# Transforms of the 3x3 convolutions' input emitted at wider gaps in a two-layer attention and convolution kernel

## The chip, the cores and the metric

The kernel runs on one core of a Trainium2 chip. The time is device microseconds of one execution; three executions of the kernel before have a median of 3188.08 us, and lie between 3178.91 and 3189.95 us. The profiled execution is a run of its own. The engines are named as the profile names them: PE is TensorE (PEld its weight loads), DVE is VectorE, ACT is ScalarE, POOL is GpSimd, SP issues the DMAs.

## What is computed

Eight images of 512 channels by 32 x 32 pixels go through two layers, in float32. Layer 0, cut to what matters here:

```python
x = x + conv_ref(gn(x))                # layer 0; gn: GroupNorm, 32 groups
t  = silu(bn(conv1x1(gn_x, cv1)))      # 512 channels, two halves of 256
ys = [t[:, :256], t[:, 256:]]
for i in range(2):                     # two blocks
    yi = ys[-1]
    z  = silu(bn(conv3x3(yi, m_cv1[i])))
    q, k, v = conv1x1(z, qkv[i])       # 4 heads of 64
    a  = softmax(q.T @ (k + r) / 8)    # over 1024 pixels
    z  = silu(bn(conv1x1(v @ a.T, m_cv2[i])))
    ys.append(yi + z)
out = silu(bn(conv1x1(concat(ys), cv2)))
```

Layer 1 is a GroupNorm and a 1x1 convolution whose weights are scaled, masked and permuted by tables; its result is added to its input.

## The kernel before

**Slots.** The work on an image's block is called here by image and block: "2_1" is image 2, block 1. The attention of one block is a slot; the slots run in the order 0_0, 1_0, 0_1, 1_1, 2_0, 3_0, 2_1, 3_1, 4_0 and so on. A slot has four units (two head pairs by two halves of the queries). A unit goes through eight key tiles t, two to a softmax step: on VectorE `soften` (L545, adds the negated maximum), on ScalarE `exponent` (L549), on GpSimd the sums (L556), on TensorE `values` (L563) of the two tiles before and `logits` (L511) of the next unit. The next unit's logits are copied out of PSUM by ScalarE (L518) and their running maximum `mx` is taken by VectorE (L523). Between two units `top` transposes mx (L531) and reduces it to `nm` (L532), `spread` writes it out into `mb` (L540); `finish` and `divide` (L577 to L586) end the unit before. A softmax step takes about 9.2 us in the trace.

**What fills TensorE between.** `slot_filler` builds a list of other work for each slot: the 3x3 convolution (`conv3`) and the projections (`project`) of the next slot, the 1x1 convolution after the attention (`conv_m2`), and a background queue (`bg`) of cv1, cv2 and layer 1 (L175, with the results cv2s and xr at L130 and L457 and x2r at L487). After each softmax step the filler runs until its share of the slot is done. A `Clock` adds up estimated costs as this work is emitted; a call placed with `clock.at(delay, f)` is emitted when the clock has passed that time. So all delays and gaps in this text are estimated us of TensorE's work, and decide only where in the program an instruction stands.

**The transform.** A 3x3 convolution is done as six products over transformed planes of four rows (`conv3`, L297 on). `transform` makes the planes from `ybuf`, the padded input, with eight VectorE instructions in this order: a (L280), b (L281), plane 1 (L282), plane 2 (L283), a2 (L285), b2 (L286), plane 3 (L287), plane 4 (L288). Planes 0 and 5 are begun on GpSimd (L343, L344) and ended on VectorE (L345, L346). The eight are handed to a `Spread`: number n is due at delay + gap x n. `conv3` forces three of them out before its first product (`upto(3)`), the fourth before the second (`upto(4)`), all before it goes on from the second product (`upto(8)`). Two calls of `transform` stand in `slot_filler`: for block 1 of the next slot (L924), and for block 0 of the slot after the next (L939). Two more, for block 0 of images 0 and 1, stand ahead of the slots, outside it.

**Orders that are kept.** `in_turn` chains the mx, the softens and the transforms on VectorE in the order in which they are emitted; `act_turn` and `pe_turn` do the same for copies and exponentials on ScalarE and for the attention's matmuls on TensorE. All other instructions are placed by the framework's own scheduling, with the same in-order queues. All matmuls of the filler and the logits share one pool of five PSUM banks (`bank`): a matmul that starts a bank waits until the one who read its contents before is done.

Of the kernel before, what the change touches and what calls it, by code (L numbers as in the profile page):

```python
# [39 lines left out]
def conv_preact_kernel(ctx: ExitStack, tc: tile.TileContext, x, cv1, cv2, mcv1, qkv, mcv2, bn, rw, rh, conv, s_in, t_in, out):  # L40
# [698 lines left out]
    slots = []  # L739
# [157 lines left out]
    def call(f, *a):  # L897
        f(*a)
        return
        yield  # L900

    def finishing(im):


        bg.add(Second(im, 0), Second(im, 1), held.pop(), Last(im, 0))
        held.append(Last(im, 1))
        bg.prepare()

    def slot_filler(s):

        prev = slots[s - 1] if s else (None, 0)
        nxt = slots[s + 1] if s + 1 < len(slots) else (None, 0)
        todo, needed = [], 0.0

        def add(us, g):
            nonlocal needed
            todo.append((us, g))
            needed += us

        im, i = nxt  # L920
        add(8.0, bg.take(8.0))
        if im and i == 1:
            add(7.0, im.conv_m2(0))
            add(0.0, call(im.transform, 1, 3.0, 1.0))  # L924
            add(9.0, bg.take(9.0))
        products = im.conv3(i) if im else iter(())
        if prev[1] == 1:
            if im:
                add(21.3, (us for _, us in zip(range(16), products)))
            add(7.0, prev[0].conv_m2(1))  # L930
            add(0.0, call(lambda: finishing(prev[0])))
        if im:
            add(10.7 if prev[1] == 1 else 32.0, products)
            add(7.0, bg.take(7.0))
        if im:
            add(21.0, im.project(i))
        if s + 2 < len(slots) and slots[s + 2][1] == 0:
            add(0.0, call(slots[s + 2][0].load_y))
            add(0.0, call(slots[s + 2][0].transform, 0, 8.0, 1.3))  # L939
        rest = SHARE - needed if im else 70.0  # L940
        if rest > 0:
            todo.append((rest, bg.take(rest, wait=True)))
        total = sum(c for c, _ in todo)
        return needed, total, todo
# [76 lines left out]
    before = None  # L1021
    for s in range(len(slots)):
        needed, total, todo = slot_filler(s)
        state = {"done": 0.0}

# [66 lines left out]
    im = images[NB - 1]  # L1092
# [55 lines left out]
```

## Time and profile before

| | us |
|---|---|
| median of three executions | 3188.08 |
| the profiled execution's own time | 3188.51 |
| its span, first to last instruction | 3186.8 |
| TensorE busy in the span | 3085.9 |
| VectorE busy | 2050.6 |
| ScalarE busy | 1717.3 |
| GpSimd busy | 1395.3 |

The mean granted TensorE clock is 0.993. The group rows that this text speaks of, from the page (busy us, mean ns of one, idle of the engine just before and who ended most of it):

```profile
L556 POOL TENSOR_TENSOR sum<-sum,st 128x256 f32<-128x256 f32 x1536 | 1126.1, 767 | 570.1 <-ACT st L549 565.0
L523 DVE TENSOR_TENSOR mx<-mx,lg 128x512 f32<-128x512 f32 x768 | 477.8, 681 | 412.2 <-ACT st L518 412.2
...
L545 DVE TENSOR_TENSOR st<-st,mb 128x1024 f32<-128x1024 f32 x512 | 603.7, 1213 | 63.6 <-PE mb L540 63.6
L313 PE MATMUL m<-plane,w_m 128*128 128x256 f32 x2304 | 537.4, 388 | 21.8 <-DVE x2r L487 9.0
```

Sixteen transforms run, of eight instructions each. Matmuls overlap in the records, so a busy TensorE isn't TensorE at its peak, and a wait counts for the time only where TensorE itself stands.

### The profile page before, as it was taken

The page shows a single profiled execution, that of the slowest core. Times are in us where ns is not written, and L with a number is a line of the kernel's source. Part 1 is how long each engine was busy: PE and PEld are TensorE (multiplying, and loading weights), DVE is VectorE, ACT ScalarE, POOL GpSimd, SP SyncE. Part 2 cuts the span into 40 slices and gives each one's busy share as a digit, 9 for nine tenths or more (in the row PEclk, how much of TensorE's full clock was granted, in tenths as well). Part 3 has the DMA queues.
Part 4 walks back from the last instruction along what each step waited for, and adds up shares of the span by engine and source line. Part 5 has one row for each costly group of instructions (what it writes and reads, how often), then busy time and mean ns, then how long its engine had stood idle before and what let it go on. Part 6 is the DMA issues. An engine that isn't in the chain of part 4 may idle for free.

```text
span 3186.8 us, 34171 instructions
## 1 busy us (share of the span) xinstructions
PE 3085.9 (97%) x11668; PEld 1522.9 (48%) x11668; DVE 2050.6 (64%) x2718; ACT 1717.3 (54%) x2347; POOL 1395.3 (44%) x1867
## 2 busy tenths in 40 slices
PE   7999999999999999999999999999999999999999
PEld 3645444454445454454445454454445454453333
DVE  5446576667666676667666676667766676666742
ACT  3255765854655555544656455554656455555631
POOL 2114444446444454445444454355434454455420
PEclk9999999999999999999999999999999999999999
DMA  8851442421233232424233332424233332413366
GB/s 294 287 187 63 154 161 83 149 79 65 88 109 129 93 119 70 148 86 137 89 109 129 119 114 75 139 83 142 90 113 132 110 122 71 145 63 129 110 212 216
DMA packets 142014, 399.35 MB, mean 125 GB/s; under 512 B 13072, under 2 KB 14352, under 8 KB 141840
## 3 DMA queue, kind: packets, MB, share of 16 engines
q1 hardware_dynamic: 141120, 396.94, 36.4%
q8 instruction: 92, 1.51, 0.2%
q14 instruction: 82, 0.67, 0.1%
q10 hardware_dynamic: 720, 0.23, 0.0%
HBM read 317.42 MB, written 79.69 MB: 125 GB/s over the span
## 4 chain that ended last, share of the span: by engine, by line
PE 70%; DVE 7%; ACT 5%; issue 3%; DMA 2%; POOL 1%; ACTq 0%; DVEq 0%; SPq 0%; POOLq 0%
PE m L313 14%; PE cv L175 12%; PE lg L511 11%; PE po L563 11%; PE qk L175 6%; PE l L175 6%; PE v L405 3%; PE m L175 2%; DVE st L545 2%; PE mb L540 2%; ACT st L518 2%; PE mt L531 2%; PE den L577 2%; DVE mx L523 1%; ACT st L549 1%
## 5 line engine op out<-in xcount | busy, mean ns | idle before, releaser
L556 POOL TENSOR_TENSOR sum<-sum,st 128x256 f32<-128x256 f32 x1536 | 1126.1, 767 | 570.1 <-ACT st L549 565.0
L523 DVE TENSOR_TENSOR mx<-mx,lg 128x512 f32<-128x512 f32 x768 | 477.8, 681 | 412.2 <-ACT st L518 412.2
L549 ACT ACTIVATE st<-st 128x1024 f32<-128x1024 f32 x512 | 539.1, 1068 | 340.2 <-DVE st L545 338.8
L518 ACT COPY st<-lg 128x512 f32<-128x512 f32 x1024 | 524.4, 596 | 351.7 <-PE lg L511 306.6
L545 DVE TENSOR_TENSOR st<-st,mb 128x1024 f32<-128x1024 f32 x512 | 603.7, 1213 | 63.6 <-PE mb L540 63.6
L313 PE MATMUL m<-plane,w_m 128*128 128x256 f32 x2304 | 537.4, 388 | 21.8 <-DVE x2r L487 9.0
L556 POOL TENSOR_TENSOR sum<-st,st 128x256 f32<-128x256 f32 x256 | 188.0, 766 | 789.4 <-ACT st L549 789.3
L563 PE MATMUL po<-st,v 128*64 128x512 f32 x2048 | 500.3, 608 | 21.7 <-ACT st L549 14.7
L511 PE MATMUL lg<-q,k 64*128 64x512 f32 x2048 | 513.7, 619 | 1.6 <-ACT y L130 1.5
L313 PEld LDWEIGHTS m<-plane,w_m 128*128 128x128 f32 x2304 | 433.0, 192 | 149.0 <-issue 44.1
L175 PE MATMUL cv<-y,w_cv 128*128 128x512 f32 x1024 | 465.4, 599 | 10.8 <-DVE mx L523 6.2
L511 PEld LDWEIGHTS lg<-q,k 64*128 64x128 f32 x2048 | 178.6, 187 | 330.1 <-issue 266.4
L175 PEld LDWEIGHTS cv<-y,w_cv 128*128 128x128 f32 x1024 | 185.7, 190 | 251.7 <-issue 227.8
L563 PEld LDWEIGHTS po<-st,v 128*64 128x64 f32 x2048 | 128.9, 137 | 327.5 <-issue 228.9
L175 PE MATMUL l<-x,w_l 128*128 128x512 f32 x512 | 235.8, 603 | 10.3 <-DVE mx L523 10.0
L175 PE MATMUL cv<-x,w_cv 128*128 128x512 f32 x512 | 233.4, 603 | 8.5 <-ACT x L165 2.4
L175 PE MATMUL qk<-z,w_qkv 128*128 128x512 f32 x512 | 234.0, 600 | 1.7 <-DVE mx L523 1.7
L584 DVE RECIPROCAL rb<-rb 128x256 f32<-128x256 f32 x128 | 215.4, 1723 | 30.6 <-ACT rb L580 30.5
L532 DVE TENSOR_REDUCE nm<-mt 128x4 f32<-128x512 f32 x128 | 82.4, 685 | 158.6 <-PE mt L531 158.5
L580 ACT COPY rb<-den 128x512 f32<-128x512 f32 x64 | 37.3, 583 | 226.9 <-PE den L577 226.9
L175 PEld LDWEIGHTS l<-x,w_l 128*128 128x128 f32 x512 | 92.7, 190 | 132.3 <-issue 107.2
L175 PEld LDWEIGHTS cv<-x,w_cv 128*128 128x128 f32 x512 | 94.3, 192 | 126.4 <-issue 107.3
(145 smaller groups left out, 2404.3 us busy)
## 6 DMA issues: line engine op xcount, KB each, us to landing
w_m<-w_m SPq DMA_DIRECT2D x96, 768.0 KB, 4.8
w_cv<-in_cv SPq DMA_DIRECT2D x90, 512.0 KB, 3.5
y<-y SPq DMA_DIRECT2D x64, 512.0 KB, 4.4
x<-in_x SPq DMA_DIRECT2D x56, 512.0 KB, 5.4
y<-y SPq DMA_DIRECT2D x64, 256.0 KB, 3.5
k<-r SPq DMA_DIRECT2D x32, 512.0 KB, 3.6
res<-y SPq DMA_DIRECT2D x32, 512.0 KB, 4.0
xr<-in_x SPq DMA_DIRECT2D x32, 512.0 KB, 4.0
```

What stands on the lines that cost most here:

```text
L175: nc.tensor.matmul(ps, w, moving, start=(n == 0), stop=(n == len(terms) - 1))
L313: nc.tensor.matmul(ps[:, ts(co, 256)].rearrange("p (t x) -> p t x", x=F), w[:, co, c, dx], u[:, 9 * c : 9 * c + 8, dx : dx + F], start=(j ...
L405: nc.tensor.matmul(ps[:, ts(j, P)], z[:, c, ts(4 * j4 + j, P)], w[:, c, 512 + P * hp : 512 + P * hp + P], start=(c == 0), stop=(c == IT - 1),)
L511: nc.tensor.matmul(lg[h], self.k[r, ts(t, P)], self.q[r, self.hp, ts(self.half, HALF)], start=True, stop=True)
L518: act_turn(nc.scalar.copy(st[:, h], lg[h]))
L523: in_turn(nc.vector.tensor_tensor(self.mx[:, h], so_far[:, h], lg[h], ALU.max))
L532: nc.vector.tensor_reduce(self.nm[:, h], mt, AX.X, ALU.max, negate=True)
L545: in_turn(nc.vector.tensor_tensor(st, st, flat(self.mb), ALU.add))
L549: act_turn(nc.scalar.activation(st, st, AF.Exp))
L556: nc.gpsimd.tensor_tensor(flat(self.acc)[:, part], flat(so_far)[:, part], st[:, part], ALU.add)
L563: nc.tensor.matmul(self.po[HD * h : HD * h + HD], self.v[:, t, ts(h, HD)], self.st[t][:, h], start=(t == 0), stop=(t == KT - 1),)
L584: nc.vector.reciprocal(self.rb[:, r], self.rb[:, r])
```

## The change

Two calls in `slot_filler` get another delay and gap. The transform of block 1 becomes due from 2.0 on at every 3.3 instead of from 3.0 on at every 1.0; that of block 0 from 8.0 on at every 3.3 instead of every 1.3. The eight instructions, what they compute and who reads them stay the same. All eight transforms of block 1 and six of block 0 (images 2 to 7) go through these calls; the two ahead of the slots are left as they were.

```diff
@@ -921,7 +921,7 @@
         add(8.0, bg.take(8.0))
         if im and i == 1:
             add(7.0, im.conv_m2(0))
-            add(0.0, call(im.transform, 1, 3.0, 1.0))
+            add(0.0, call(im.transform, 1, 2.0, 3.3))
             add(9.0, bg.take(9.0))
         products = im.conv3(i) if im else iter(())
         if prev[1] == 1:
@@ -936,7 +936,7 @@
             add(21.0, im.project(i))
         if s + 2 < len(slots) and slots[s + 2][1] == 0:
             add(0.0, call(slots[s + 2][0].load_y))
-            add(0.0, call(slots[s + 2][0].transform, 0, 8.0, 1.3))
+            add(0.0, call(slots[s + 2][0].transform, 0, 8.0, 3.3))
         rest = SHARE - needed if im else 70.0
         if rest > 0:
             todo.append((rest, bg.take(rest, wait=True)))
```

## The prediction

> **What bounds the kernel now.** I read the page's engine table first, then TensorE's list of waits, then the timeline and the table by stretch at each place where a moved transform runs.
>
> ```profile
> span 3186.8 us, 34171 instructions
> PE 3085.9 (97%) x11668; PEld 1522.9 (48%) x11668; DVE 2050.6 (64%) x2718; ACT 1717.3 (54%) x2347; POOL 1395.3 (44%) x1867
> ```
>
> TensorE is busy for 3085.9 of 3186.8 us. No matmul is added or removed, so what the change can win is part of the 100.9 us in which TensorE stands, plus matmuls that run at a lower clock. Who ends those waits:
>
> ```profile
> PE po L563 <- ACT st L549: 14.7, 12, 3.7
> ...
> PE l L175 <- DVE mx L523: 10.0, 5, 2.6
> PE m L313 <- DVE x2r L487: 9.0, 3, 3.5
> PE cv L175 <- DVE mx L523: 8.2, 7, 2.0
> PE m L313 <- ACT cv2s L130: 8.2, 3, 2.8
> ```
>
> (us in total, times, longest.) None of these is a wait for a transform's own plane. They are waits for PSUM banks that ScalarE or VectorE has not read out yet. The timeline around image 2, block 1 shows why (start, duration):
>
> ```profile
> 1136.49 1.14 DVE L280 SCALAR_TENSOR_TENSOR a<-ybuf 128x544 f32<-128x544 f32 x1
> ...
> 1137.55 1.25 DVE L281 SCALAR_TENSOR_TENSOR b<-ybuf 128x544 f32<-128x544 f32 x1
> ...
> 1138.83 1.14 DVE L282 TENSOR_TENSOR plane<-a,b 128x544 f32<-128x544 f32 x1
> ...
> 1139.88 0.71 DVE L283 TENSOR_TENSOR plane<-a,b 128x544 f32<-128x544 f32 x1
> ...
> 1140.52 2.34 DVE L545 TENSOR_TENSOR st<-st,mb 128x1024 f32<-128x1024 f32 x2
> ...
> 1141.76 1.06 ACT L549 ACTIVATE st<-st 128x1024 f32<-128x1024 f32 x1 [7.13 <-DVE st L545]
> ...
> 1142.84 1.28 ACT L130 ACT_TABLE_LOAD   x1
> ...
> 1144.13 0.78 ACT L130 ACTIVATE cv2s<-cv,bn_b,bn_s 128x512 f32<-128x512 f32 x1
> ...
> 1144.96 1.43 PE L313 MATMUL m<-plane,w_m 128*128 128x256 f32 x3 [2.71 <-ACT cv2s L130]
> ```
>
> Four transform instructions stand ahead of soften (L545). ScalarE has idled 7.13 us for it, then does the exponential, a table load and the activation that frees the bank; TensorE waits 2.71 us. The same pattern with other last steps stands at image 3, block 1, and image 4, block 0:
>
> ```profile
> 1333.24 3.07 PE L313 MATMUL m<-plane,w_m 128*128 128x256 f32 x13 [1.90 <-DVE x2r L487]
> ...
> 1457.88 2.41 PE L175 MATMUL l<-x,w_l 128*128 128x512 f32 x5 [1.83 <-DVE mx L523]
> ```
>
> And at image 3, block 0, where L287 and L288 stand ahead of the soften:
>
> ```profile
> 908.24 3.27 PE L175 MATMUL cv<-y,w_cv 128*128 128x512 f32 x7 [1.46 <-DVE mx L523]
> ```
>
> A long stall can cost twice. Three stretches from the table by stretch (us, busy times, then PEclk, the granted clock):
>
> ```profile
> 1862.00:1869.00 7.00, 6.22 (x15) 5.00 (x16) 5.58 (x9) 5.00 (x7) 4.71 (x5) 0.51 0.52 162
> 2053.00:2056.40 3.40, 3.40 (x10) 2.67 (x9) 2.03 (x4) 1.82 (x3) 3.30 (x6) 0.52 0.05 20
> ...
> 2583.00:2590.00 7.00, 6.14 (x32) 5.45 (x33) 5.88 (x10) 5.65 (x9) 4.71 (x5) 1.00 0.52 170
> ```
>
> The first and the last are the same stage for images 4 and 6, with nearly the same stall (2.87 and 2.78 us); after one the clock is half for about 6.8 us, after the other it is full. A half-clock stretch of 3.4 us loses about 1.7 us.
>
> **What the Trainium skill says.** "TensorE: Matmul & The Clock Gate", Part 1, "What's actually happening": the array falls to half clock after an idle window of about 3.4 us and rises after a busy one, and the window runs freely. The trace agrees with stretches of 3.4 and 6.8 us, and with images 4 and 6 differing; but here single stalls of 2.4 to 3.7 us already do it, sometimes, and among the moved places no single one of 2.1 us or less did (image 2's cluster below did). "PSUM — Partial Sum Buffer", "Engine vs sequencer instructions": the queues of ScalarE and VectorE are strictly first in, first out. The chain above is that. "SBUF — State Buffer", "Who interferes with whom": VectorE and GpSimd share one port pair as an exclusive lock. In the trace L286 takes 712 ns at the least and 1248 ns at the most, and the slow ones lie beside GpSimd's sums. "ScalarE: Activation LUTs", "What ACT_TABLE_LOAD costs": about 1283 ns and a drain; the trace has 1.28 us.
>
> **The change part by part.** Nothing is added or removed on any engine; SP's order is the same, so no DMA moves in its queue. GpSimd's list changes at one L343, at image 2. Of 16 transforms, 14 move: all eight of block 1, and block 0 of images 2 to 7. VectorE's order by program, image 2 block 1: before, L280 L281 L282 L283, soften 6, 7, L285 L286; after, L280 L281, soften 6, 7, L282, xr, then the four mx, L283 L285 L286 and the two nm. So each transform instruction that leaves the front of a soften brings it 0.71 (alone) to 1.25 us (beside sums) forward. A "stall" below is TensorE's lost time against its pitch, which is up to 0.2 us more than the idle in brackets.
>
> - *Images 2, 4, 6, block 1.* Stalls 2.78, 2.87, 2.78. L282 and L283 (1.14 + 0.71, less overlap) leave the chain: cv2s ends about 1.7 us earlier, 1.1 us of stall stays. 3 x 1.7 = 5.0. A stall of 1.1 should no longer drop the clock: 1.7 (image 2) and 3.4 (image 4), of which I take 3.4, as the window runs freely. Together 8.4.
> - *Images 3, 5, 7, block 1.* A first stall (2.40, 2.76, 1.71), ended by the mx behind ScalarE's norms, stays. The second (2.06, 3.71, 3.71) waits for x2r behind L285 to L288 and soften. After, L285 to L288 follow the four mx, and the program has this matmul wait for mx of step 6 instead, which should end about 1330.0 to 1330.7 against 1331.2 wanted at image 3, and up to 0.8 late at images 5 and 7. 2.06 + 2.9 + 2.9 = 7.9, with two half-clock stretches (2 x 1.65 = 3.3): 11.2. x2r is then needed one product later, 24 matmul records or 5.4 us, about 2.6 us after it is there.
> - *Images 4, 6, block 0.* 1.99 and 2.00: soften 4 (now at 1454.33 behind L285, L286, x2r, L287, L288) comes by 1450.9; mx then ends at 1455.6 at the latest against 1455.9 wanted. 4.0.
> - *Images 3, 5, 7, block 0.* 1.62, 1.63, 1.64 go for the same reason. But ScalarE's order turns there: the exponential of step 2 now precedes the table load and cv2s, which ends about 896.65 (before 892.76), while TensorE wants that bank at 895.66: a new stall of 1.0. Bounds -1 and +1.6 each; I take +0.6, so 1.9 in all.
> - *Image 0, block 1.* 1.65: mx should end at 439.3 against 439.05: 1.3. *Image 1, block 1.* 1.41, held by ScalarE's last activation, where one norm moves behind it: 0.4 (0 to 0.7).
> - *Image 2, block 0* (728 to 750). TensorE has too little work here: stalls of 1.36, 1.19 and 1.87 and half clock from 742.4 to 749.2. Soften 4 comes about 1.75 us earlier, soften 6 about 3 us. Bounds 1 and 6.5 (1.19 + 1.87 + 3.4); I take 4.0.
>
> Sum 8.4 + 11.2 + 4.0 + 1.9 + 1.3 + 0.4 + 4.0 = 31.2 us. What the moved instructions newly stand ahead of: in block 1 three or four of L283 to L288 now stand between the last mx and nm (L532). At image 3 VectorE's mx ends at 1335.57 and nm starts at 1339.38, and mb (L540), which needs nm, at 1342.35. Four at 1.25, x2r 0.63 and the small group-norm steps (about 1.1) fill 6.7 us, from an mx that ends near 1332.2: nm is done at 1340.2, and mb, 2.06 earlier than before, is wanted at 1340.3. The cover just suffices at the slow pace; at the quick pace 2 us are over. I cost it at nothing. The planes themselves have 3 us or more.
>
> The profiled execution took 3188.51 us for its span of 3186.8, and stands 0.43 over the median of 3188.08. 3188.5 - 31.2 = 3157.3; against the median 3157.
>
> **The rivals.** *The stalls move rather than go.* ScalarE's table loads and copies become last: each soften comes early, and its bank is still late, as at images 3, 5, 7, block 0. For it: the first stalls of images 3, 5, 7, block 1 already end so. Against: ScalarE idled 7.13 us before the exponential above. Only a third of the sum stays, about 10: 3178.
>
> *All go, with the lower clock.* The stalls listed are 8.4 + 9.5 + 4.0 + 4.9 + 1.65 + 1.41 + 4.4 = 34.3, half clock 5.1 + 3.3 + 3.4 = 11.8: 46 us, 3142. Against it: the table load stays in the chain.
>
> *Slower: a late nm.* In the eight block-1 windows L283 to L288 delay nm, so mb, and with it the whole next soften chain; the cover computed above was 0.1 us at the slow pace. If mx itself ends 2.5 us later than I think, each window loses 2.5 us, and with 6.8 us at half clock (3.4) 5.9: 8 x 5.9 = 47 against the 31 won, so +16: 3204. It decides from where nm ends more than 2 us later against mb than worked out. Against: before, VectorE idled 158.5 us over 128 nm.
>
> *The change doesn't do what it says.* conv3 forces three, then four, then all of the transform's instructions out (upto), which could undo the spacing. By the program's order it does not: no burst of more than three is left directly ahead of a soften. No change, 3188.
>
> **How the numbers follow.** Forecast (22 to 40 us won) 0.56; stalls move 0.24, of which a third still passes the bound; all go 0.12; slower 0.06; no effect 0.02. About 0.5% (16 us) is what a measurement of this kernel can tell from none: the three runs spread over 11 us. Faster 0.56 + 0.12 + 0.08 = 0.76, within 0.18, slower 0.06. The range 3138 to 3181 takes in the forecast, the larger gain and most of the moved stalls.
>
> **What would show it.** Right: soften 6 some 1.7 us earlier at image 2, block 1, with TensorE's wait near 1.1; "m L313 <- DVE x2r L487" gone from the waits; the waits of l and cv for mx down by 4 and 5; no half clock after 1862, 2053 and 2770; TensorE's idle near 78 us. Wrong: new waits of cv for cv2s over 1 us at images 3, 5, 7; waits of mb for nm; half clock at new places.

## The result, and the profile after

| | before | changed |
|---|---|---|
| median of six executions, us | 3188.59 | 3160.7 |
| lowest and highest | 3178.91, 3189.95 | 3156.5, 3164.71 |
| span of the profiled execution | 3186.8 | 3160.4 |
| TensorE busy | 3085.9 | 3078.6 |

The changed kernel takes 0.9918 of the time (95% interval 0.9907 to 0.993), 27.9 us less. Of the span's 26.4 us, 7.3 are TensorE's busy time (above all matmuls that no longer run at half clock) and 19.1 its idle time. TensorE's waits in the changed kernel (us in total, times, longest):

```profile
PE po L563 <- ACT st L549: 19.9, 17, 3.7
...
PE l L175 <- DVE mx L523: 6.0, 3, 2.3
PE cv L175 <- ACT cv2s L130: 4.6, 6, 0.8
PE cv L175 <- DVE mx L523: 4.5, 4, 2.7
...
PE m L313 <- ACT cv2s L130: 2.7, 3, 0.9
...
PE po L563 <- DVE mx L523: 0.8, 2, 0.4
```

The wait of m for x2r, 9.0 before, is gone; l and cv for mx fell from 10.0 to 6.0 and from 8.2 to 4.5; m for cv2s from 8.2 to 2.7. Two rows grew by more than 2 us: cv for cv2s, from 2.3 to 4.6, and po for the exponential, from 14.7 to 19.9. The second is mostly a change of name: po for mx fell from 6.9 to 0.8, and the two together from 21.6 to 20.7. Two rows of before that the comparison needs:

```profile
PE po L563 <- DVE mx L523: 6.9, 8, 2.3
...
PE cv L175 <- ACT cv2s L130: 2.3, 3, 0.8
```

The timeline at image 2, block 1, in the changed kernel:

```profile
1137.65 1.24 DVE L281 SCALAR_TENSOR_TENSOR b<-ybuf 128x544 f32<-128x544 f32 x1
...
1138.82 2.34 DVE L545 TENSOR_TENSOR st<-st,mb 128x1024 f32<-128x1024 f32 x2
1140.06 1.06 ACT L549 ACTIVATE st<-st 128x1024 f32<-128x1024 f32 x1 [5.33 <-DVE st L545]
...
1142.43 0.78 ACT L130 ACTIVATE cv2s<-cv,bn_b,bn_s 128x512 f32<-128x512 f32 x1
...
1143.26 3.08 PE L313 MATMUL m<-plane,w_m 128*128 128x256 f32 x13 [0.91 <-ACT cv2s L130]
```

Soften begins at 1138.82 instead of 1140.52, cv2s at 1142.43 instead of 1144.13: 1.70 us earlier each, and TensorE waits 0.91 us where it waited 2.71. The table by stretch at the two places of before that were shown at half clock (us, busy times of the five engines, then the granted clock, DMA share and GB/s):

```profile
1851.00:1858.00 7.00, 6.93 (x36) 6.15 (x37) 6.92 (x9) 4.88 (x8) 4.21 (x5) 1.00 0.73 227
2036.00:2039.40 3.40, 3.40 (x17) 2.86 (x16) 3.37 (x6) 0.63 (x1) 2.63 (x3) 1.00 0.90 275
```

Both have the full clock, and do 36 and 17 matmul records where half clock did 15 and 10. The next table is made from the start of the same matmul in both traces (TensorE runs the same matmuls, in the same order but for a few at image 2, block 0): how much a stretch of slots got shorter (-) or longer (+). The last column is a second profiled execution of the changed kernel (the ninth run below).

| stretch | forecast | first profile | second |
|---|---|---|---|
| images 2, 4, 6, block 1 | -8.4 | -8.6 | -7.7 |
| images 3, 5, 7, block 1 | -11.2 | -11.4 | -13.3 |
| images 4, 6, block 0 | -4.0 | -4.2 | -4.2 |
| images 3, 5, 7, block 0 | -1.9 | -2.7 | -1.3 |
| image 0, block 1 | -1.3 | -1.6 | -1.3 |
| image 1, block 1 | -0.4 | +0.3 | -0.7 |
| image 2, block 0 | -4.0 | -2.0 | -1.5 |
| all 14 places | -31.2 | -30.2 | -30.0 |
| ahead of the first moved transform | 0 | +4.2 | +3.5 |
| after the last | 0 | -0.6 | +5.4 |

Ahead of the first moved transform the two programs are the same, so the 4.2 us there are the spread between executions (the other profiles below stand between -0.6 and +8.7 there, against the same profile of before, and all eleven at +3.2 on the mean). Where the 5.4 of the last line come from is told at the end.

### The profile page after: what moved, and what is told of

Its sections match the earlier page's. It is cut to its first block, busy times and chain, and to the rows that moved or that the text cites. A ratio compares the mean times of both kernels' runs of the same rounds, so it can differ in the third digit from the quotient of the medians.

```text
span 3160.4 us, 34182 instructions
## 1 busy us (share of the span) xinstructions
PE 3078.6 (97%) x11668; PEld 1515.6 (48%) x11668; DVE 2041.5 (65%) x2718; ACT 1718.7 (54%) x2347; POOL 1398.7 (44%) x1867
## 4 chain that ended last, share of the span: by engine, by line
PE 75%; ACT 4%; DVE 3%; issue 2%; DMA 2%; POOL 1%; ACTq 0%; DVEq 0%; SPq 0%; POOLq 0%
PE cv L175 14%; PE m L313 13%; PE lg L511 12%; PE po L563 12%; PE l L175 7%; PE qk L175 6%; PE v L405 3%; PE m L175 3%; PE den L577 2%; PE mb L540 2%; PE mt L531 1%; ACT st L518 1%; POOL sum L556 1%; ACT st L549 1%; DVE st L545 1%
## 5 line engine op out<-in xcount | busy, mean ns | idle before, releaser
L313 PE MATMUL m<-plane,w_m 128*128 128x256 f32 x2304 | 528.7, 383 | 4.7 <-ACT cv2s L130 2.7
L563 PE MATMUL po<-st,v 128*64 128x512 f32 x2048 | 498.9, 605 | 20.7 <-ACT st L549 19.9
L313 PEld LDWEIGHTS m<-plane,w_m 128*128 128x128 f32 x2304 | 426.5, 189 | 129.0 <-issue 45.4
L175 PE MATMUL cv<-y,w_cv 128*128 128x512 f32 x1024 | 464.5, 599 | 8.6 <-ACT cv2s L130 4.6
L175 PEld LDWEIGHTS cv<-y,w_cv 128*128 128x128 f32 x1024 | 185.8, 190 | 248.9 <-issue 226.7
L175 PE MATMUL cv<-x,w_cv 128*128 128x512 f32 x512 | 235.6, 607 | 9.2 <-DVE mx L523 2.7
L175 PE MATMUL l<-x,w_l 128*128 128x512 f32 x512 | 236.5, 606 | 6.2 <-DVE mx L523 6.0
L175 PE MATMUL qk<-z,w_qkv 128*128 128x512 f32 x512 | 234.0, 600 | 1.3 <-DVE mx L523 1.3
L175 PEld LDWEIGHTS cv<-x,w_cv 128*128 128x128 f32 x512 | 95.0, 193 | 128.8 <-issue 107.6
L175 PEld LDWEIGHTS l<-x,w_l 128*128 128x128 f32 x512 | 93.1, 191 | 127.9 <-issue 110.3
```

The source lines that it names most:

```text
L175: nc.tensor.matmul(ps, w, moving, start=(n == 0), stop=(n == len(terms) - 1))
L313: nc.tensor.matmul(ps[:, ts(co, 256)].rearrange("p (t x) -> p t x", x=F), w[:, co, c, dx], u[:, 9 * c : 9 * c + 8, dx : dx + F], start=(j ...
L563: nc.tensor.matmul(self.po[HD * h : HD * h + HD], self.v[:, t, ts(h, HD)], self.st[t][:, h], start=(t == 0), stop=(t == KT - 1),)
```

## The experiments

Two theories went in. S: a transform instruction ahead of a soften delays by its length the exponential, the PSUM bank and the matmul behind it, and each place stands alone. Against it M (the stalls only move from engine to engine), D (the burst itself costs, wherever it stands), and, after the first four runs, A (ScalarE's order of cv2s and the exponential decides). "Soften 6" is the soften of key tile 6. Ratios are against the kernel before on the same chip. Stalls are counted as in the prediction, against TensorE's pitch (the usual time from one matmul's start to the next): 0.98 us is the stall where a bracket shows 0.91 of idle.

**One call at a time.** Each kernel is the kernel before with one of the two edits:

```diff
-            add(0.0, call(im.transform, 1, 3.0, 1.0))
+            add(0.0, call(im.transform, 1, 2.0, 3.3))
```

> Only the block-1 call has the new delay and gap (2.0, 3.3). Theory S (a transform instruction ahead of a soften delays the exponential, the bank and the matmul behind it, and each place stands alone): the block-1 places alone, about 21 us won against before (ratio 0.9934); stalls of images 2, 4, 6 near 1.0 instead of 2.8, the x2r waits of images 3, 5, 7 gone, and unchanged: 1.99 and 2.00 at images 4 and 6, block 0, and three of 1.6 at images 3, 5, 7, block 0. Rival M (the stalls move, and only the two edits together pay, since a later slot catches up): under 12 us won.

```diff
-            add(0.0, call(slots[s + 2][0].transform, 0, 8.0, 1.3))
+            add(0.0, call(slots[s + 2][0].transform, 0, 8.0, 3.3))
```

> Only the block-0 call has the new gap (8.0, 3.3). Theory S: about 9 us won (ratio 0.9972): the two stalls of 2.0 gone, the three of 1.6 gone against three new ones of 0.85 where cv2s comes late, 2 us at image 2; the block-1 stalls of 2.8 and 2.1 to 3.7 as before. Rival M: none or a loss, since the late cv2s at images 3, 5, 7 takes back what is won.

Block 1 alone: 3168.0 us against 3190.64, ratio 0.9931 (0.9911 to 0.995), 22.6 us won where S expected 21. Block 0 alone: 3182.21, ratio 0.9978 (0.9969 to 0.9986), 8.4 us won where it expected 9. The two ratios multiply to 0.9909, beside 0.9918 for both together: the parts add up, and M falls. With block 1 alone the x2r waits are gone and the stalls of 1.99 at images 4 and 6, block 0, stay; with block 0 alone the reverse. One detail missed: with block 1 alone the cv2s stalls of images 4 and 6 are 1.70, not 1.0. That does not belong to this edit: the changed kernel has the same 1.70 at image 6 in its second profile. There the additions that fill `ybuf` (L430) end 0.7 us later than in the first, counted from the mx before them, and with them a, b and soften.

**The burst, later.** The gaps of before, both bursts five later:

```diff
-            add(0.0, call(im.transform, 1, 3.0, 1.0))
+            add(0.0, call(im.transform, 1, 8.0, 1.0))
-            add(0.0, call(slots[s + 2][0].transform, 0, 8.0, 1.3))
+            add(0.0, call(slots[s + 2][0].transform, 0, 13.0, 1.3))
```

> The gaps of before (1.0 and 1.3), but both bursts begin five later (8.0 and 13.0), so that the burst stands behind soften 6, 7 at images 2, 4, 6 of block 1, and still five instructions ahead of soften 6 at images 3, 5, 7 and of soften 4 at images 4, 6 of block 0. Theory S (place against the soften counts, not the density): the cv2s stall of images 2, 4, 6 gone, but plane 1 is then late behind the four mx, so a wait of m for L282 of 3 us or more in its place; images 3, 5, 7 of block 1 and images 4, 6 of block 0 keep stalls of 2 us or more. Time within 15 us of before. Rival D (the density itself costs: a burst runs at the slow pace beside GpSimd's sums, wherever it stands): the stalls of images 2, 4, 6 stay with the same releaser, cv2s.

3210.2 us, ratio 1.0059 (1.0042 to 1.0075): 19.6 us slower, more than the 15 allowed. The timeline of this kernel, at image 2, block 1:

```profile
1155.21 0.73 DVE L282 TENSOR_TENSOR plane<-a,b 128x544 f32<-128x544 f32 x1
...
1156.04 6.24 PE L313 MATMUL m<-plane,w_m 128*128 128x256 f32 x20 [4.21 <-ACT st L549]
```

The bracket names ScalarE, but the matmul starts at 1156.04, 0.10 us after plane 1 (L282) ends at 1155.94: the first product needs plane 1, which now stands behind the four mx. The wait for cv2s has gone as S has it, and one for the plane has come. Images 3, 5, 7 have five transform instructions ahead of soften 6 and stalls of 5.9 to 6.4 us. D expected the wait for cv2s to stay; it didn't.

**All eight at once.**

```diff
-            add(0.0, call(im.transform, 1, 3.0, 1.0))
+            add(0.0, call(im.transform, 1, 3.0, 0.0))
-            add(0.0, call(slots[s + 2][0].transform, 0, 8.0, 1.3))
+            add(0.0, call(slots[s + 2][0].transform, 0, 8.0, 0.0))
```

> Gap 0 in both calls: all eight instructions at one place, begun where the kernel before begins them. Theory S: four more instructions, 2.9 to 5.0 us, ahead of soften 6 at images 2, 4, 6 of block 1: stalls of 5.7 to 7.8 us there; at images 4, 6 of block 0 soften 4 is free, so the 2.0 goes, but soften 2 is 4 to 7 us later and a wait appears one step earlier; the same at images 3, 5, 7 of block 1, where the x2r wait goes and the wait of l for mx grows. Sum 15 to 45 us slower than before. Rival M (TensorE waits for the end of each transform, however it is placed): the same time as before within 8 us.

3190.36 us, ratio 0.9999 (0.9988 to 1.001). S is wrong here: no stall of 5.7 to 7.8 us, and the waits of m for cv2s and for x2r are gone. ScalarE's and TensorE's timelines of this kernel, image 2, block 1, show why:

```profile
1155.92 0.78 ACT L130 ACTIVATE cv2s<-cv,bn_b,bn_s 128x512 f32<-128x512 f32 x1 [2.58 <-PE cv L175]
...
1161.85 1.06 ACT L549 ACTIVATE st<-st 128x1024 f32<-128x1024 f32 x1 [3.85 <-DVE st L545]
```

```profile
1159.60 5.45 PE L313 MATMUL m<-plane,w_m 128*128 128x256 f32 x24
1166.11 1.26 PE L531 MATMUL mt<-ident,mx 128*128 128x128 f32 x8 [1.06 <-DVE mx L523]
```

With soften so late, the program has cv2s ahead of the exponential on ScalarE. cv2s follows the matmuls that fill its bank directly, the product starts without a wait, and only the transposes of mx wait, 1.06 us. This suggests that what stands ahead of soften costs TensorE through ScalarE's order, and that this order is a second lever; the next runs test it. The cost moved: po waits for exponentials, 14.7 us before, for 32.9 here. The time is the one that rival M named, but not for the reason it gave: no product waits for a plane in this profile.

**ScalarE's order alone.** cv2s is not in the chain that `act_turn` writes out. One edit puts it there, where it is emitted, ahead of the exponential of the same step:

```diff
-                    bn_silu(t, ps, BN_CV2 + co)
+                    act_turn(nc.scalar.activation(t, ps, AF.Silu, bias=bn_b[:, BN_CV2 + co : BN_CV2 + co + 1], scale=bn_s[:, BN_CV2 + co : BN_CV2 + co + 1]))
```

First on the kernel before, no transform moved:

> The transforms stand where the kernel before has them; alone the activation cv2s (L456) is put into ScalarE's written order, so that it stands ahead of the exponential of the same step. Theory A (the stalls of images 2, 4, 6, block 1, come from the order on ScalarE: the exponential, which waits for soften, stands ahead of the table load and cv2s): the three cv2s stalls of 2.8 us gone or under 1 without any transform moved, 8 to 13 us won there with the half clock, less up to 4 us for six more table loads; the x2r waits of images 3, 5, 7 (2.1 to 3.7), the 2.0s of images 4, 6 and the 1.6s of images 3, 5, 7, block 0, stay. Ratio 0.997 to 0.999. Theory S (the transform ahead of the soften is the cause whatever ScalarE's order): stalls of 2 us or more stay there, ratio 1.000 or more.

3181.02 us against 3187.37, ratio 0.9977 (0.9969 to 0.9985). Image 2, block 1, in this kernel (ScalarE, then TensorE):

```profile
1139.78 0.78 ACT L456 ACTIVATE cv2s<-cv,bn_b,bn_s 128x512 f32<-128x512 f32 x1 [1.62 <-PE cv L175]
...
1142.98 1.06 ACT L549 ACTIVATE st<-st 128x1024 f32<-128x1024 f32 x1 [1.12 <-DVE st L545]
```

```profile
1143.46 4.80 PE L313 MATMUL m<-plane,w_m 128*128 128x256 f32 x21
```

The exponential still waits for soften, which still stands behind four transform instructions, but cv2s is done 2.4 us before it, and the product starts without a wait. So it is at images 4 and 6: all three cv2s stalls are gone. Instead the transposes of mx stall there by 0.8 to 1.3 us and mb by 0.8, and the x2r stalls of 3.7 us stay. Theory A holds for these places, and S only as long as ScalarE has the exponential ahead of cv2s. Then on the changed kernel:

> The changed kernel with the same edit. Theory A: the remaining 0.98s of images 2, 4, 6 and the new 0.85s of images 3, 5, 7, block 0, go, 5.5 us won against the changed kernel (about 3155), less what six more table loads of 1.28 us cost if they come onto the path (up to 7.7). Theory S: the 0.98s and 0.85s stay, no gain.

3150.52 us, ratio 0.9885 (0.9868 to 0.9902). ScalarE and TensorE at image 2, block 1, in this kernel:

```profile
1139.05 0.78 ACT L456 ACTIVATE cv2s<-cv,bn_b,bn_s 128x512 f32<-128x512 f32 x1 [1.62 <-PE cv L175]
...
1141.14 1.06 ACT L549 ACTIVATE st<-st 128x1024 f32<-128x1024 f32 x1
```

```profile
1142.72 5.45 PE L313 MATMUL m<-plane,w_m 128*128 128x256 f32 x24
```

ScalarE loads the table for cv2s at 1136.14, while it would wait for the convolution anyway; the exponential comes some 0.6 us later than in the changed kernel (0.33 us after the logits' start at 1140.81; there 0.31 ahead of 1140.37); and the product starts without a wait. The stalls of 0.85 at images 3, 5, 7, block 0, are gone too, and of the six added table loads TensorE sees little: its wait of cv for m2s is 3.4 us in four places instead of 2.1 in one.

**Other gaps.** 5.0, then 2.0, in both calls, with the changed kernel's delays:

```diff
-            add(0.0, call(im.transform, 1, 2.0, 3.3))
+            add(0.0, call(im.transform, 1, 2.0, 5.0))
-            add(0.0, call(slots[s + 2][0].transform, 0, 8.0, 3.3))
+            add(0.0, call(slots[s + 2][0].transform, 0, 8.0, 5.0))
```

> Gap 5.0 in both calls, else as the changed kernel; ScalarE's order is that of the changed kernel. Theory S with late planes: one instruction fewer ahead of soften 6 at images 2, 4, 6, but plane 1 (L282) stands behind the four mx and is 4 to 5 us late for the first product: waits of m for L282 of 3 to 5 us at images 2, 4, 6 of block 1, and planes 3 and 4 behind soften 0, 1 and the divides are late by 1 to 3 us at images 3, 5, 7. 15 to 30 us slower than the changed kernel, about the time of before. Rival (the further apart the better): as fast as the changed kernel or faster.

> Gap 2.0 in both calls, with the changed kernel's delays. Theory S: three instructions ahead of soften 6 at images 2, 4, 6 (two in the changed kernel, four before): stalls of 1.7 to 2.1; at images 4, 6 of block 0 three and x2r stand ahead of soften 4: about 1.5; x2r waits of 1 to 2.5 at images 3, 5, 7. 8 to 18 us won against before (0.9944 to 0.9975). Rival (only the step from four to two counts): the time of before within 5 us.

Gap 5.0: 3187.75 us, ratio 1.0 (0.9988 to 1.0011): the whole gain is given back. Its timeline at image 2, block 1:

```profile
1153.59 0.72 DVE L282 TENSOR_TENSOR plane<-a,b 128x544 f32<-128x544 f32 x1
...
1154.41 5.93 PE L313 MATMUL m<-plane,w_m 128*128 128x256 f32 x19 [4.61 <-ACT st L549]
```

Again the product starts 0.10 us after plane 1 ends. Stalls of 4.0 to 5.4 us stand at all five such places, images 1, 2, 4, 6 of block 1 and image 2 of block 0; those for planes 3 and 4 at images 3, 5, 7 did not come.

Gap 2.0: 3179.57 us, ratio 0.9976 (0.9968 to 0.9985), 7.8 us won (4.8 to 10.2 by the interval) where S expected 8 to 18 and its rival less than 5, so the time alone does not decide between them. Two rows of its waits:

```profile
PE m L313 <- ACT cv2s L130: 6.2, 3, 2.1
...
PE mb L540 <- DVE nm L532: 4.9, 5, 1.6
```

The stalls do decide. At images 2, 4, 6, with three instructions ahead of soften 6, the stall is 2.15; with two (the changed kernel) 0.98, with four (before) 2.78: each one counts. At images 3, 5, 7 x2r still stands behind soften and TensorE idles 3.5 us for it, more than the 1 to 2.5 expected: there it is not the number that counts, but whether the program lets the first product wait for mx and only the second for x2r. The stalls of about 1.5 expected at images 4 and 6, block 0, did not come. And a wait came that nobody expected here: at images 2 and 6 of block 1 mb idles 1.31 us for nm, behind L285 to L288.

In block 1 the change moves the delay too, from 3.0 to 2.0. With the delay of 2.0 the gaps 2.0, 3.3 and 5.0 win 7.8, 27.9 and nothing, so the delay alone does not make the gain; 3.0 with gap 3.3 was not run.

**Both kernels again, side by side on one chip.**

> The changed kernel again, beside the next run on the same chip: ratio to before 0.9907 to 0.993 as measured; cv2s stalls of 0.98 at images 2, 4, 6 and of 0.85 at images 3, 5, 7, block 0.

> The changed kernel with cv2s ahead of the exponential, again, on the same chip as the run above. Theory A: 0.15 to 0.35% faster than the changed kernel beside it (ratio to before 0.987 to 0.990), and the 6.3 us wait of gv_b at 3023 us was chance (GpSimd's sums in the way of one small VectorE instruction): absent here, with a profiled time near 3150. Rival: the wait belongs to the order, comes again, and the gain over the changed kernel is within the spread.

The changed kernel 3160.56 us (0.9915, 0.9901 to 0.9929); with cv2s first 3152.51 (0.9892, 0.9876 to 0.9908), 8.0 us less. The intervals overlap, so the gain over the changed kernel rests on two batches that agree (3150.5 and 3152.5 against 3160.7 and 3160.6), and on 26 of the 30 pairs of executions on this chip. The changed kernel with cv2s first is thus the fastest of all that were run. The stalls of 0.98 came again at images 2 and 4 and were 1.70 at image 6; those of 0.85 came again at all three places; and the wait of gv_b at 3023 us is absent from the second profile of the kernel with cv2s first, as expected for chance.

## Why the prediction was right

*The sum.* 31.2 us forecast, 30.2 and 30.0 in the two profiles for the 14 places; the medians moved by 27.9, to 3160.7 where 3157 was forecast. The forecast was made from one profile of before. Ahead of the first moved transform that profile is 3.2 us quicker than the mean of the other eleven, and yet its whole time is the median's; so it probably lost as much to chance further on, and the 14 places owe part of their 30 us to it. That is an estimate from these profiles; the medians themselves can't show it. That the sum comes out closer than its terms is in part luck: single terms are off by up to 2.5 us, with both signs, and half clock left some stalls and came to others.

*Images 2, 4, 6, block 1.* Right to 0.1: soften and cv2s 1.70 earlier, a stall of 0.98 where 1.1 was forecast (1.70 at image 6 in the second profile), no half clock there. The chain as written (soften, exponential, table load, cv2s) held in the kernel as it stood. What the forecast did not see is that its first link is not needed: the fifth run breaks the chain at ScalarE and takes the stall away without moving a transform.

*Images 3, 5, 7, block 1.* The x2r wait is gone, as forecast, because the program has the first product wait for mx. The single terms differ more than their sum: the first stall became 1.71, 2.42 and 2.39 (2.40, 2.76 and 1.71 before), and half clock came after the first stalls of images 5 and 7 as the one at image 3 went. In the second profile they are 1.72, 2.44 and 1.44, with half clock at image 5 alone. The forecast let two half-clock stretches go and expected no new ones; that three went and two or one came is chance, and "half clock at new places" was one of its signs of being wrong. The same chance made image 1, block 1, longer in the first profile: 3.4 us at half clock from about 614 on, which neither the profile of before nor the second one has.

*Images 4, 6 and 3, 5, 7, block 0.* -4.2 for 4.0; the new stall for cv2s was forecast as 1.0 and is 0.85, in the trace as "cv L175 <- ACT cv2s", which rose from 2.3 to 4.6.

*Image 2, block 0.* The term that was mis-sized: 4.0 forecast, 2.0 and 1.5 measured, within its bounds of 1 and 6.5. The half clock from 742.4 went, as forecast. From the first wait of po (728.46 before, 731.42 in the changed kernel) to the products behind the logits (748.90, 746.98) the stretch is 4.9 us shorter, in the second profile 4.4. But then a new wait takes part of it back. TensorE's timeline in the changed kernel:

```profile
750.12 1.26 PE L531 MATMUL mt<-ident,mx 128*128 128x128 f32 x8 [1.58 <-DVE mx L523]
```

Before, the same transposes (at 751.76) did not wait at all; in the second profile this wait is 1.58 too. From the transposes to the next logits another 1.3 us are lost in both profiles; there den, the matmul of the sums that ends a unit, now waits for GpSimd. 4.9 - 1.6 - 1.3 is the 2.0 of the table. TensorE has too little other work there, so a stall that goes brings the next one nearer.

*What was costed at nothing.* The late nm: in the changed kernel at image 3, block 1, L285 to L288 stand between mx and nm, and no new wait of mb followed, in either profile. That holds for this gap only: with gap 2.0 the same four stand between mx and nm at image 2, block 1, and mb waits 1.31 us. The row "mb <- nm" of the waits grew from 0.7 to 2.3, but 1.6 of it is at 401 us, ahead of the first moved transform. Of the rival "the stalls move" 0.85 three times and some 3 us at image 2, block 0, came true, no more; "all go" fails at the stalls that ScalarE ends. A loss against the changed kernel came with gap 5.0 and with the later burst, and mainly for another reason than the one forecast: plane 1, not nm.

## What to carry to other kernels

Where one engine is busy 97% of the time, list its stalls one by one, name the last link of each chain and see how far the change moves that link: here the sum of such small terms came out within 4% in two profiles and 12% above the medians, while single terms missed by more. A helper's work on an in-order queue has a window, not a best distance: ahead of a step that the next engine needs before it can free a buffer it costs its length, too far behind it its own reader waits. And look at the order of the engine between the two: putting one activation ahead of another on ScalarE took away three stalls that looked like VectorE's.

## What the runs showed of the hardware that was not expected

A VectorE instruction of 128 x 4 elements took 9.26 us in the sixth run's profile, and 0.16 us where nothing disturbs it. Timelines of VectorE and of GpSimd in that profile:

```profile
3013.70 9.26 DVE L150 TENSOR_TENSOR gd_b<-mv_b,gms_b 128x4 f32<-128x4 f32 x1
```

```profile
3006.48 16.47 POOL L556 TENSOR_TENSOR sum<-sum,st 128x256 f32<-128x256 f32 x24 [1.74 <-ACT st L549]
```

It ends as a row of 24 sums without a gap on GpSimd ends. The Trainium skill, "SBUF — State Buffer", "Who interferes with whom", calls the port pair that the two engines share an exclusive lock; a single sum takes some 0.7 us, so here VectorE did not get its turn between one sum and the next, for nine microseconds of them, and TensorE waited 6.25 us for it. In the first profile of the changed kernel VectorE did get its turn: there the same instruction stands at 3021.91, inside a like row of sums, and took 0.63 us. It is chance: in the second profile of the changed kernel it took 8.93 us (TensorE waited 5.9 us for it, which is behind the +5.4 of the table). In the two profiles of the kernel with cv2s first it took 9.26 and at most 1.1; of twelve profiles three have it.
